# 250 blocks instead of 252 in a graph attention kernel: block bounds chosen from two candidates, expert groups of three first and two last, the fallback's branch behind the last addition

## The chip, the core and the metric

The kernel runs on one core of one Trainium2 chip. Times are device microseconds of one execution; lower is better. A core has TensorE (PE, matmuls, with weight loads of its own), VectorE (DVE), ScalarE (ACT), GpSimd (POOL) and SyncE (SP, which here issues nearly all plain transfers). Each engine works through its own instructions in order, and they meet at semaphores.

## The reference

One layer: graph attention with relation types over 30000 nodes of 256 features and 510000 edges (480000 random ones and a loop at each node), and after it a mixture of experts. The edges come sorted by destination.

```python
feat_all = einsum('ni,rhid->rnhd', layernorm(x), conv_weights)   # 8 relations, 4 heads of 64
el = sum(feat_all[type, src] * attn_l[type]);  er = sum(feat_all[type, dst] * attn_r[type])
e = leaky_relu(el + er, 0.2)
alpha = softmax of e over the edges of one destination
h[dst] = sum(alpha * feat_all[type, src]) + h_bias
x = x + h
y = layernorm(x)
out = x + shared_mlp(y) + sum of the 2 best of 4 experts, weighted by a softmax of their gates
```

## The kernel before, in words

There are two stages and a fallback.

Stage 1 goes over 235 tiles of 128 rows. Each is normalised, turned, and multiplied by the weights of all relations and heads (`group`, L304, six PSUM buffers); the rows go to `feat` in device memory, with the source half of the score as a 65th column of each head. Between these matmuls the program places side work, a step at a time: the generator `edge_records` (packs edges into records and finds the bounds of the blocks), then `places` (prepares each block's indices and flags, in batches of 12 blocks), then the loads of the experts' weights. `aside()` takes one step per row tile while `edge_records` runs and two afterwards. From row tile 178 on `first_rows` gathers one row per partition of each block ahead (L632) and stores these to `stage`, at a pace spread over the remaining tiles and never ahead of what `places` has made ready.

Stage 2 goes over `NBLK + 1` blocks. A block owns whole nodes: all edges of at most 128 nodes, and at most `CAP` = 2048 edges, 16 for each partition. Block t begins at the first node whose edges begin at or after `t * S`, found in a window of `WN` = 64 edges (L433 to L440: `miss` marks edges of the same node as the one before, a minimum finds the first other one). The last block, t = NBLK, is different: it takes the last 18 x 128 edges and the last 128 nodes. `bad` gathers the cases in which this doesn't hold (a block with too many edges or nodes, edges not sorted, and others).

The order of stage 2 is written by hand: t counts blocks, and each t has six slots, c = 0 to 5. In slot 0 of t come the loads of block t + 2 and the gathers of block t + 1: 15 indirect transfers (18 in the last block), issued by POOL at L962, into a ring `ft` of four blocks. Block t itself has its scores in slot 1 (L1066), the ends of its rows turned in slot 2 (L993), a scan across partitions (L1084), turned back (L1091), and softmax and exponentials in slot 5 (L1107). In the next t its rows are weighed (L1115) and summed by matmuls with one-hot matrices (`sums`, L1122), and `finish` divides by the denominator (`den`, L1144). In slot 0 of t + 2 `residual_sum` adds x (L1157) and takes the statistics of the second layernorm (L739).

The experts work on groups of `T` = 4 blocks. When a group's last block is added, its steps (`Experts.steps`) go to the end of the list `todo`, and each slot takes one of them, two from t = NBLK on. The steps are `spread` (L744), two `scale` (L749 to L754), two `turn` (L762), `shared1` and `gates`, four `experts1`, `shared2`, two `experts2`, two `weigh`, `turn_gates`, and one `last` for each block of the group (L871 to L877: matmuls into a PSUM tile with one buffer, the addition that ends the block, and its output transfer). What a step returns is called `late` and runs before the next step. With 253 blocks there are 62 groups of four, then one of three, then one of two.

After stage 2 comes the fallback, a slower method for inputs that don't fit: three loops (L1224, L1300, L1414) whose count is a multiple of `again`, read from `bad` at L1222. With `bad` = 0 they run zero times. `bad` is complete in stage 1, and each engine passes these loops at the place where the program puts them among its instructions.

Of the kernel before, what the change touches and what calls it, by code (L numbers as in the profile page):

```python
# [10 lines left out]
F32 = mybir.dt.float32  # L11
# [10 lines left out]
P = 128  # L22
# [11 lines left out]

U = 16
CAP = U * P
S = 2016
UL = 18  # L40
T = 4

# [14 lines left out]
def kernel(  # L57
# [48 lines left out]
    thr_d = dram.tile([NBLK, 2, P], F32, name="thr_d")  # L106
    exc_d = dram.tile([P], F32, name="exc_d")
    KT = -(-(NBLK + 1) // P)
    lo_d = dram.tile([KT, P], F32, name="lo_d")
    n_d = dram.tile([KT, P], F32, name="n_d")  # L110
    uns_d = dram.tile([EP], F32, name="uns_d")
    mnmx = dram.tile([2, NGRP], F32, name="mnmx")
    lohi_d = dram.tile([NT, 2], I32, name="lohi_d")

# [9 lines left out]
    nbc = const.tile([P, NBLK], F32, name="nbc")  # L124
    rowid = const.tile([P, NBLK + 1], F32, name="rowid")
    bad = const.tile([1, 1], I32, name="bad")
    lohi = const.tile([1, NT * 2], I32, name="lohi")
    hb = const.tile([P, D], F32, name="hb")

# [91 lines left out]
    with ExitStack() as cx:  # L221
# [123 lines left out]
        def edge_records(cl):  # L345
# [11 lines left out]
            for c in range(nch):  # L357
# [8 lines left out]
                else:  # L366
                    nc.vector.memset(d_sb[:, 0:1], -1)
                    nc.sync.dma_start(d_sb[:, 1:], dstv[:, :n])
                    with nc.allow_non_contiguous_dma(reason="one edge of each partition, once"):
# [32 lines left out]
                              zx.bitcast(BF16)[:, :R * 3 * H])  # L402
            yield


            WN = 64
            FAR = float(1 << 23)
            dw = gp.tile([P, KT, WN + 1], I32, name="dw")
            nc.gpsimd.memset(dw, -1)
            jj = gp.tile([P, WN], F32, name="jj")  # L410
            nc.gpsimd.iota(jj, pattern=[[1, WN]], base=0, channel_multiplier=0,
                           allow_small_or_imprecise_dtypes=True)
            first = gp.tile([P, KT], F32, name="first")
            irow = gp.tile([P, 1], F32, name="irow")
            nc.gpsimd.iota(irow, pattern=[[0, 1]], base=0, channel_multiplier=1,
                           allow_small_or_imprecise_dtypes=True)
            yield
            for k in range(KT):
                nc.vector.tensor_scalar(first[:, k:k + 1], irow, float(S), float(k * P * S), op0=ALU.mult,
                                        op1=ALU.add)  # L420
            nc.sync.dma_start(dw[0:1, 0, 1:], dst[0:WN].rearrange("(o c) -> o c", o=1))
            for k in range(KT):
                a = 1 if k == 0 else 0
                n = min(P, NBLK + 1 - k * P)
                nc.sync.dma_start(dw[a:n, k, :],
                                  bass.AP(tensor=dst.tensor, offset=dst.offset + (k * P + a) * S - 1,
                                          ap=[[S, n - a], [1, WN + 1]]))
            before_last = gp.tile([1, 1], I32, name="before_last")
            nc.sync.dma_start(before_last, dst[E - UL * P - 1:E - UL * P].rearrange("(o c) -> o c", o=1))
            yield  # L430
            lof = gp.tile([P, 2, KT], F32, name="lof")
            miss = gp.tile([P, KT, WN], F32, name="miss")
            nc.vector.tensor_tensor(miss, dw[:, :, 1:], dw[:, :, :WN], op=ALU.is_equal)  # L433
            yield
            for i, v in enumerate((jj[:, None, :].to_broadcast([P, KT, WN]), dw[:, :, 1:])):
                cand = gp.tile([P, KT, WN], F32, name="cand")
                nc.vector.scalar_tensor_tensor(cand, miss, FAR, v, op0=ALU.mult, op1=ALU.add)
                nc.vector.tensor_reduce(lof[:, i, :], cand, AX.X, ALU.min)
                yield
            nc.vector.tensor_add(lof[:, 0, :], lof[:, 0, :], first)  # L440
            nc.vector.tensor_scalar_min(lof[:, 0, :], lof[:, 0, :], float(E))
            nc.vector.tensor_scalar(lof[:, 1, :], lof[:, 1, :], 0.0, float(N), op0=ALU.max, op1=ALU.min)
            yield
            lor = gp.tile([1, KT * P], F32, name="lor")
            nr = gp.tile([1, KT * P], F32, name="nr")
            with nc.allow_non_contiguous_dma(reason="first edges and nodes of blocks, once"):
                for i, (t_d, row) in enumerate(((lo_d, lor), (n_d, nr))):
                    nc.sync.dma_start(t_d.rearrange("k p -> p k"), lof[:, i, :])
                    yield
                    if i:  # L450
                        nc.sync.dma_start(t_d[0:1, 0:1], zx[0:1, 0:1])
                        yield
                    nc.sync.dma_start(row, t_d.rearrange("(o k) p -> o (k p)", o=1))
                    yield
            nc.vector.tensor_copy(lo_sb, lor)
            nc.vector.tensor_copy(n_sb, nr)
            nc.vector.tensor_scalar_min(n0_sb, nr, float(N - P))
# [1 line left out]
            yield  # L459
            nc.vector.tensor_scalar(rowid[:, :NBLK], nbc, irow, None, op0=ALU.add)  # L460
            nc.vector.tensor_scalar_add(rowid[:, NBLK:], irow, float(N - P))
            unm = gp.tile([EP, 1], F32, name="unm")
            nc.vector.tensor_reduce(unm, uns, AX.X, ALU.max)
            yield
            with nc.allow_non_contiguous_dma(reason="one number of each partition, once"):
                nc.sync.dma_start(uns_d.rearrange("(p o) -> p o", o=1), unm)
            yield
            unr = gp.tile([1, EP], F32, name="unr")
            nc.sync.dma_start(unr, uns_d.rearrange("(o p) -> o p", o=1))


            two = gp.tile([1, 5], F32, name="two")
            gap = gp.tile([1, NBLK], F32, name="gap")
            for i, (row, most) in enumerate(((lor, CAP), (nr, P))):
                nc.vector.tensor_sub(gap, row[:, 1:NBLK + 1], row[:, :NBLK])
                nc.vector.tensor_reduce(two[:, i:i + 1], gap, AX.X, ALU.max)
# [4 lines left out]
            yield  # L481
            nc.vector.tensor_reduce(two[:, 4:5], unr, AX.X, ALU.max)
            nc.vector.tensor_reduce(bad, two, AX.X, ALU.max)

        BT = 3 * NT // 4
        count = {"ready": 0, "sent": 0}
# [395 lines left out]
    with ExitStack() as cx:  # L882
# [241 lines left out]

        groups = {}

        left, sizes = (NBLK + 1) % T, [T] * ((NBLK + 1) // T)
        sizes = sizes[:-1] + [T - 1, 2] if left == 1 else sizes + [left] if left else sizes[:-1] + [2, 2]
        member = [(sum(sizes[:q]), n) for q, n in enumerate(sizes) for _ in range(n)]
        todo = []  # L1130
        late = []
# [17 lines left out]
        def residual_sum(t):  # L1149
            s = blk.pop(t)  # L1150
            q, n = member[t]
            j = t - q
            if j == 0:
                x1 = x1p.tile([P, T, D], F32, name="x1")
                groups[q] = Experts(xc, ph_p, pc_p, x1, n, lambda i, r, q=q: put(q + i, r))
            x1 = groups[q].x1
            nc.vector.tensor_add(x1[:, j, :], s.ho.rearrange("p h d -> p (h d)"), s.xt)  # L1157
            groups[q].stats(j)
            if j == n - 1:
                todo.extend(groups.pop(q).steps())  # L1160

        with tc.manual_schedule():
            for t in range(-2, NBLK + 12):
                if t == 0:
                    for fb in fbs:
                        nc.vector.memset(fb, 0.0)

                def at(f, b, *a):  # L1170
                    if 0 <= b <= NBLK:
                        f(b, *a)
                for c in range(NCH):
                    while late:
                        late.pop()()
                    if c == 0:
                        at(load, t + 2)
                        at(gather, t + 1)
                        at(flags, t + 1)
                    if c == 1:  # L1180
                        at(flags_across, t + 1)
                    if c == 2:
                        at(turn_ends, t)
                    if c == 3:
                        at(across, t)
                    if c == 4:
                        at(turn_back, t)
                    if c == 5:
                        at(softmax, t)
                        at(exps, t)  # L1190
                        at(dest_pick, t + 2, 0)
                    if c == 4:
                        at(dest_select, t + 2)
                    if c < NCH - 1:
                        at(weigh, t - 1, c + 1)
                    if 0 < c < 4:
                        at(dest_pick, t + 1, c)
                    if c == 0:
                        at(residual_sum, t - 2)
                    if c == 1:  # L1200
                        at(scores, t)
                    for _ in range(2 if t >= NBLK else 1):
                        while late:
                            late.pop()()
                        if todo:
                            after = todo.pop(0)()
                            if after:
                                late.append(after)
                    if c == 5:
                        at(weigh, t, 0)  # L1210
                    if c == 4:
                        at(dest_expand, t + 2, 0)
                    if c < 3:
                        at(dest_expand, t + 1, c + 1)
                    at(onehot, t, c)
                    at(sums, t - 1, c)
                    if c == 5:
                        at(finish, t - 1)
            assert not todo and not groups and not late


    again = nc.values_load(bad[0:1, 0:1], min_val=0, max_val=1)  # L1222
    with tc.tile_pool(name="gr2", bufs=1) as gp, tc.tile_pool(name="ed2", bufs=2) as ep:
        with tc.For_i(0, again):  # L1224
            mn = gp.tile([EP, GPP], F32, name="mn")
# [228 lines left out]
```

## Time and profile before

| | us |
|---|---|
| median of three runs (lowest, highest) | 8487.05 (8483.83, 8509.22) |
| the profiled execution | 6603.28 |
| its span, first to last instruction | 6601.5 |
| PE busy in the span | 6047.9 (92%) |
| DVE busy | 5254.8 (80%) |
| POOL busy | 4082.8 (62%) |
| ACT busy | 3405.3 (52%) |
| mean granted clock of TensorE | 0.971 |

The runs are longer than the profiled execution by 1884 us. The profile describes the latter alone.

A row of a group gives line, engine, operation, tiles, and after the bar its busy time, the mean time of one in ns, and the idle time of the engine before it with what ended it. In a timeline the columns are start, duration, engine and line, and in brackets the idle time before and what ended it. `issue` is time in which the engine waited for nothing that the profile shows. A letter q behind an engine's name (POOLq) is its queue, where branches, semaphores and transfers are issued; these don't count as busy.

### The profile page before, as it was taken

How to read it: one execution, taken by the hardware profiler on the slowest of the kernel's cores; microseconds unless marked ns; L12 is line 12 of the kernel's file. 1: busy time of each engine (PE TensorE's matmuls, PEld its weight loads, DVE VectorE, ACT ScalarE, POOL GpSimd, SP SyncE). 2: the span in 40 equal slices, each digit the busy share in tenths (PEclk: the TensorE clock that was granted, in tenths of full speed). 3: DMA queues.
4: the chain of work that ended last, by engine and by line, in shares of the span. 5: the costliest groups of instructions: out<-in, count | busy, mean ns of one | idle time of the engine just before them, and what ended most of it. 6: DMA issues, size and time to landing. Idle time of an engine off the chain costs nothing. (4 is left out here: it accounts for less than half of the span.)

```text
span 6601.5 us, 97367 instructions
## 1 busy us (share of the span) xinstructions
PE 6047.9 (92%) x25770; PEld 3891.0 (59%) x25771; DVE 5254.8 (80%) x13699; ACT 3405.3 (52%) x8758; POOL 4082.8 (62%) x4424
## 2 busy tenths in 40 slices
PE   9999999999689989989899998899899999988998
PEld 5555555555356666666666666666666666666665
DVE  5555767644488888898888898898888888888895
ACT  2222222222256566666666665666656666566664
POOL 1111111266677777777777777777777777777773
PEclk9999999999899999999999999999999999999998
DMA  6666676799855555555555555555555555555552
GB/s 228 226 210 200 226 238 225 247 337 330 267 160 163 161 164 163 163 163 160 165 163 163 160 164 165 163 160 161 164 162 167 158 163 164 163 165 159 163 163 74
DMA packets 764586, 1214.72 MB, mean 184 GB/s; under 512 B 242498, under 2 KB 602917, under 8 KB 733813
## 3 DMA queue, kind: packets, MB, share of 16 engines
q1 hardware_dynamic: 568581, 668.72, 31.4%
q0 software_dynamic: 194400, 539.40, 29.3%
q8 instruction: 209, 3.42, 0.2%
q14 instruction: 356, 2.92, 0.1%
q10 hardware_dynamic: 1040, 0.26, 0.0%
HBM read 821.54 MB, written 386.43 MB: 183 GB/s over the span
## 5 line engine op out<-in xcount | busy, mean ns | idle before, releaser
L962 POOL DMA_INDIRECT ft<-feat,rk x3798 | 3606.7, 950 | 1169.0 <-issue 390.3
L1122 PE MATMUL po<-ft,oh 128*128 128x260 f32 x8100 | 2189.0, 407 | 137.1 <-DVE ho L1147 128.6
L1122 PEld LDWEIGHTS po<-ft,oh 128*128 128x128 f32 x8100 | 1520.4, 201 | 433.8 <-issue 196.5
L304 PE MATMUL ps<-w,xT 128*128 128x448 f32 (+1 forms) x4700 | 1708.4, 519 | 2.0 <-DMA w<-_L_gnn_conv_weights_dram 2.0
L1115 DVE TENSOR_TENSOR ft<-ft,p 128x768 f32<-128x768 f32 x1518 | 1292.2, 852 | 90.0 <-ACT ft L1108 86.1
L1049 ACT ACTIVATE oh<-icol,rk 128x128 f32<-128x128 f32 x4032 | 1327.7, 389 | 0.0
L304 PEld LDWEIGHTS ps<-w,xT 128*128 128x128 f32 x4700 | 875.6, 190 | 689.1 <-issue 603.3
L306 ACT COPY fo<-ps 128x448 f32<-128x448 f32 (+1 forms) x711 | 378.0, 533 | 1062.5 <-PE ps L304 972.5
L1050 ACT ACTIVATE oh<-oh 128x384 f32<-128x384 f32 x1518 | 741.1, 488 | 48.1
L1026 PEld LDWEIGHTS <-ohT 128*128 128x128 bf16 x4050 | 378.2, 158 | 408.9 <-issue 332.6
L1039 DVE TENSOR_REDUCE e<-ere 128x16 f32<-128x384 f32 (+1 forms) x1012 | 561.3, 555 | 34.6
L1037 DVE TENSOR_TENSOR ere<-pe,rk 128x384 f32<-128x384 f32 x1008 | 550.8, 546 | 1.3 <-PE pe L1026 1.3
L1107 ACT ACTIVATE p<-e 128x64 f32<-128x64 f32 (+1 forms) x253 | 70.2, 277 | 839.2 <-DVE e L1061 808.1
L1026 PE MATMUL pe<-erp,ohT 128*128 128x96 bf16 x4050 | 438.8, 233 | 60.5 <-DVE ohT L1009 37.5
L818 PE MATMUL ph<-xT,v 128*128 128x512 f32 (+2 forms) x1024 | 490.3, 602 | 0.4 <-ACT a L819 0.4
L306 DVE COPY fo<-ps 128x448 f32<-128x448 f32 (+1 forms) x464 | 242.3, 527 | 200.4 <-PE ps L304 194.1
L293 DVE COPY xT<-ptr 128x256 f32<-128x256 f32 x229 | 97.0, 424 | 368.6 <-PE ptr L291 367.0
L632 POOL DMA_INDIRECT fr<-feat,lowc x252 | 239.7, 951 | 193.7 <-DMA stage<-fr 90.2
L1009 DVE TENSOR_SCALAR ohT<-dr,rowid 128x2064 bf16<-128x2064 int16 (+1 forms) x253 | 323.6, 1279 | 19.8 <-DMA stage<-fr 19.7
L273 POOL TENSOR_TENSOR xb<-xg,hb 128x1024 f32<-128x1024 f32 (+1 forms) x59 | 140.7, 2385 | 272.1 <-DMA xg<-in_x_dram 161.9
L993 PE MATMUL t<-ident,fb 128*8 128x128 f32 x506 | 104.3, 290 | 214.9 <-DVE fb L1072 214.7
L819 ACT ACTIVATE a<-ph,c 128x512 f32<-128x512 f32 (+2 forms) x256 | 173.6, 678 | 195.7 <-PE ph L818 195.7
(219 smaller groups left out, 6810.9 us busy)
## 6 DMA issues: line engine op xcount, KB each, us to landing
feat<-fo SPq DMA_DIRECT2D x234, 1040.0 KB
dr<-dk_d SPq DMA_DIRECT2D x252, 516.0 KB
ft<-feat,rk POOLq DMA_INDIRECT x3798
stage<-fr SPq DMA_DIRECT2D x84, 390.0 KB
ft<-stage SPq DMA_DIRECT2D x252, 130.0 KB
xt<-xb_d SPq DMA_DIRECT2D x253, 128.0 KB
out_dram<-og SPq DMA_DIRECT2D x253, 128.0 KB
xb_d<-xb SPq DMA_DIRECT2D x58, 512.0 KB
```

Of the source, the lines that this page charges most:

```text
L304: nc.tensor.matmul(ps, t["xT"][:, k, :], w[:, k, c0:c1], start=k == 0, stop=k == 1)
L306: eng(t["fo"][:, h0:h1, :HD], ps[:, :n].rearrange("p (a d) -> p a d", d=HD))
L818: nc.tensor.matmul(ps[:, :self.w], lhs, rhs, start=i == 0, stop=i == len(pairs) - 1)
L962: nc.gpsimd.indirect_dma_start(out=s.ft[:, u].rearrange("p h d -> p (h d)"), out_offset=None, in_=feat[:, :], in_offset=bass.IndirectOffse ...
L1009: nc.vector.tensor_scalar(ohT[:, :3 * s.dw].rearrange("n (i e) -> n i e", i=3), s.dr[:, :, :s.dw], rowid[:, t:t + 1], None, op0=ALU.is_equal)
L1026: nc.tensor.matmul(pe[:, u - u0].rearrange("p f r -> p (f r)"), s.ov[:, u, :], s.erp.rearrange("n h k r -> n (h k r)"), start=True, stop=True)
L1037: nc.vector.tensor_mul(ere, s.pe[:, :u1 - u0], s.th[:, u0:u1, None, :].to_broadcast([P, u1 - u0, H * 3, R]))
L1039: nc.vector.tensor_reduce(s.e[:, :, u0:u1].rearrange("p h u -> p u h"), ere.rearrange("p u (h k) r -> p u h (k r)", h=H), AX.X, ALU.add)
L1049: nc.scalar.activation(s.oh[:, u, :], icol, AF.Abs, bias=s.nd[:, u:u + 1])
L1050: nc.scalar.activation(s.oh[:, u0:u1], s.oh[:, u0:u1], AF.Relu, bias=1.0, scale=-1.0)
L1115: nc.vector.tensor_mul(fc, fc, pc[:, :, None].to_broadcast([P, (u1 - u0) * H, HD]))
L1122: nc.tensor.matmul(s.po.rearrange("n h d -> n (h d)"), s.oh[:, u, :], s.ft[:, u].rearrange("p h d -> p (h d)"), start=u == 0, stop=u == s. ...
```

## The change

`S`, the distance of the blocks' nominal starts, goes from 2016 to 2032, so `NBLK` from 252 to 250.

The bounds are found in another way. The window now reaches 64 edges back too, and there are two candidates for each bound, the last start of a node before `t * S` and the first at or after it. A scan over the blocks (`late`) takes the later one where the block before it still fits, and the earlier one otherwise. The candidates go through device memory once, as four rows (`cand_d`), in place of two round trips for `lo_d` and `n_d`, and the choice is made on one partition. The tiles of this part are in a pool of their own that is closed at its end; the generator has more steps.

The groups of the experts are sized the other way round: what is left over comes first (a group of three with 251 blocks), then fours, then two groups of two. Two steps per slot are taken in t = NBLK - 2, NBLK - 1, NBLK and from NBLK + 2 on, and one in NBLK + 1. When the last block is added, the first three steps of its group (`spread` and both `scale`) go ahead of what is still in `todo`. From t = NBLK on, what a step returns is held until the next step is taken rather than run at the slot's start.

At the end of stage 2 VectorE copies `bad` to `redo`, behind its last addition, and `again` is read from `redo`.

```diff
-S = 2016
+S = 2032
@@ edge_records
-            dw = gp.tile([P, KT, WN + 1], I32, name="dw")
+            dw = bp.tile([P, KT, 2 * WN + 1], I32, name="dw")
...
-            nc.vector.tensor_tensor(miss, dw[:, :, 1:], dw[:, :, :WN], op=ALU.is_equal)
-            yield
-            for i, v in enumerate((jj[:, None, :].to_broadcast([P, KT, WN]), dw[:, :, 1:])):
-                cand = gp.tile([P, KT, WN], F32, name="cand")
-                nc.vector.scalar_tensor_tensor(cand, miss, FAR, v, op0=ALU.mult, op1=ALU.add)
-                nc.vector.tensor_reduce(lof[:, i, :], cand, AX.X, ALU.min)
-                yield
+            nc.vector.tensor_tensor(miss, dw[:, :, 1:], dw[:, :, :2 * WN], op=ALU.is_equal)
+            yield
+            for i, v in enumerate((jj[:, None, :].to_broadcast([P, KT, 2 * WN]), dw[:, :, 1:])):
+                for f, (far, op) in enumerate(((-FAR, ALU.max), (FAR, ALU.min))):
+                    w2 = slice(f * WN, (f + 1) * WN)
+                    cand = bp.tile([P, KT, WN], F32, name="cand")
+                    nc.vector.scalar_tensor_tensor(cand, miss[:, :, w2], far, v[:, :, w2], op0=ALU.mult, op1=ALU.add)
+                    nc.vector.tensor_reduce(lof[:, i, f, :], cand, AX.X, op)
+                    yield
...
+                for k in range(4):
+                    nc.sync.dma_start(cand_d[k].rearrange("k p -> p k"), lof[:, k // 2, k % 2, :])
+                    yield
+                yield
+                nc.sync.dma_start(cands.rearrange("o i k -> o (i k)"),
+                                  cand_d.rearrange("(o i) k p -> o (i k p)", o=1))
...
+            for f in range(2):
+                for i, most in enumerate((CAP, P)):
+                    gap = bp.tile([1, NBLK], F32, name="gap")
+                    nc.vector.tensor_sub(gap, cands[:, 2 * i + 1, 1:NBLK + 1], cands[:, 2 * i + f, :NBLK])
+                    if i == 0:
+                        nc.vector.tensor_scalar(may[:, f], gap, float(most), None, op0=ALU.is_le)
+                    else:
+                        nc.vector.scalar_tensor_tensor(may[:, f], gap, float(most), may[:, f], op0=ALU.is_le,
+                                                       op1=ALU.mult)
+                yield
+            nc.vector.tensor_scalar_add(may[:, 1], may[:, 1], -1.0)
...
+            nc.vector.tensor_tensor_scan(late[:, 1:NBLK + 1], may[:, 1], may[:, 0], 1.0, ALU.add, ALU.max)
...
+            for i, row in enumerate((lor, nr)):
+                nc.vector.tensor_sub(row, cands[:, 2 * i + 1], cands[:, 2 * i])
+                nc.vector.tensor_mul(row, row, late)
+                nc.vector.tensor_add(row, row, cands[:, 2 * i])
+                yield
+            nc.sync.dma_start(n_d.rearrange("(o k) p -> o (k p)", o=1), nr)
...
@@ groups
-        left, sizes = (NBLK + 1) % T, [T] * ((NBLK + 1) // T)
-        sizes = sizes[:-1] + [T - 1, 2] if left == 1 else sizes + [left] if left else sizes[:-1] + [2, 2]
+        left = (NBLK + 1) % T
+        sizes = [left] * (left > 0) + [T] * ((NBLK + 1) // T - 1) + [2, 2]
...
-                todo.extend(groups.pop(q).steps())
+                steps = groups.pop(q).steps()
+                if t == NBLK:
+                    todo[:0] = steps[:3]
+                    steps = steps[3:]
+                todo.extend(steps)
...
-            for t in range(-2, NBLK + 12):
+            for t in range(-2, NBLK + 6):
...
+                steps = 2 if NBLK - 2 <= t != NBLK + 1 else 1
                 for c in range(NCH):
-                    while late:
+                    while late and t < NBLK:
                         late.pop()()
...
-                    for _ in range(2 if t >= NBLK else 1):
+                    for _ in range(steps):
...
             assert not todo and not groups and not late
-    again = nc.values_load(bad[0:1, 0:1], min_val=0, max_val=1)
+            nc.vector.tensor_copy(redo, bad)
+    again = nc.values_load(redo[0:1, 0:1], min_val=0, max_val=1)
```

## The prediction, made before the changed kernel had run

> **What bounds the kernel now.** First I read the busy times of the engines stretch by stretch, because the page's shares average two stages with different limits. The columns are PE, weight loads, DVE, ACT, POOL (busy us, instructions in brackets), granted clock, DMA share, GB/s.
>
> ```profile
> 400.00:600.00 200.00, 200.00 (x604) 108.69 (x603) 106.49 (x317) 51.62 (x110) 17.04 (x24) 1.00 0.58 186
> 1400.00:1600.00 200.00, 200.00 (x603) 108.63 (x602) 95.72 (x282) 51.48 (x109) 125.69 (x124) 1.00 0.96 330
> 3000.00:4000.00 1000.00, 902.56 (x4325) 616.50 (x4325) 888.61 (x2291) 621.37 (x1639) 757.17 (x798) 0.97 0.57 162
> 4000.00:5000.00 1000.00, 904.74 (x4315) 617.22 (x4313) 887.83 (x2278) 621.08 (x1638) 757.13 (x798) 0.97 0.57 163
> ```
>
> Up to about 1730 us (projection to feat) PE has no gap. In the block stage PE and DVE stand at 90% and 89%, POOL at 76% only, and yet POOL is the bound. That shows in the groups by line and in POOL's timeline:
>
> ```profile
> L962 POOL DMA_INDIRECT ft<-feat,rk x3798 | 3606.7, 950 | 1169.0 <-issue 390.3
> ```
>
> ```profile
> 1750.34 0.94 POOL L962 DMA_INDIRECT ft<-feat,rk  x1 [12.04 <-DMA erp<-erp_d]
> 1751.59 0.95 POOL L962 DMA_INDIRECT ft<-feat,rk  x1 [0.30 <-issue]
> ...
> 6511.85 0.95 POOL L962 DMA_INDIRECT ft<-feat,rk  x1 [0.31 <-issue]
> 6513.10 0.95 POOL L962 DMA_INDIRECT ft<-feat,rk  x1 [0.30 <-issue]
> ```
>
> Each gather is 0.95 us and is followed by 0.30 us that no buffer causes: whichever engine is named as releaser, the gap is 0.30. From 1750.34 to 6514.05 us 3798 gathers run without a hole, (6514.05 - 1750.34) / 3798 = 1.254 us each. A block of 15 gathers is 18.8 us. So blocks, not matmuls, set this stage, and 87.5 us (6601.5 - 6514.05) come after the last gather.
>
> Third, the timeline of that tail:
>
> ```profile
> 6558.65 0.16 DVE L1144 TENSOR_SCALAR den<-po 128x4 f32<-128x4 f32 x1 [3.79 <-PE po L1122]
> ...
> 6562.39 0.43 DVE L739 BATCH_NORM_STATS2 c_st<-x 128x6 f32<-128x256 f32 x1 [2.25 <-SPq L1224]
> ...
> 6565.24 0.15 DVE L749 RECIPROCAL c_rs<-c_rs 128x2 f32<-128x2 f32 x1
> ...
> 6591.66 2.07 PE L873 MATMUL pf<-v,a 128*128 128x256 f32 x4 [5.75 <-issue]
> ...
> 6594.92 0.42 DVE L877 TENSOR_TENSOR og<-pf,x 128x256 f32<-128x256 f32 x1 [9.77 <-PE pf L874]
> 6595.38 0.36 SPq L1139 DMA_DIRECT2D out_dram<-og  x1
> ```
>
> The loops of the fallback (L1224, L1300, L1414, run zero times) stand inside the last block's chain: DVE waits 2.25 us at the first, PE 5.75 us at the second. In the records of lines, PE's own branch of L1300 lasts 3748 ns.
>
> **What the Trainium skill says.** "Runtime: NRT & Kernel Launch", section Instruction fetch mechanics: fetching is sequential, and a taken branch to a far target waits for a fetch. The 3748 ns agrees. "TensorE: Matmul & The Clock Gate", Part 1: after an idle window of about 3.4 us TensorE falls to half clock until it has been busy as long. The trace agrees: granted clock is 1.00 until 6560, 0.50 from 6565 to 6575, 0.79 and 1.00 after it, and 0.50 again from 6590, each time behind a branch.
>
> **The change part by part**, against the profiled execution (span 6601.5 us, 6603.28 with what lies around it).
>
> *Two blocks fewer.* S from 2016 to 2032 makes ceil((510000 - 2048) / S) 250 instead of 252. That is 30 gathers x 1.254 = -37.6 us on the bounding queue. Work of other engines goes too and was covered. The gathers behind `stage` are two fewer, beside PE's full stage 1; their pace is spread over the same row tiles, so their end stays: 0 (+-2).
>
> *Bounds.* A block may hold 2048 edges. I worked the rules out on the reference's seeded `dst`. The old rule at S = 2032 would overfill 5 blocks, up to 2052 edges; the new one moves 7 boundaries back and its largest block has exactly 2048 edges and 126 nodes, so the fallback isn't taken. The cost is on DVE in stage 1: two more pairs on 128x128 elements (about 0.28 per operation, L433), and on one partition eight operations for `may`, one addition, six for `lor` and `nr`, 0.40 each (L475, L476), and a scan of some 0.7 (L572 takes 0.57 for 204 elements): 1.1 + 6.0 + 0.7 = about 8 us. DVE is half idle there and PE full with six PSUM buffers in flight: cost 0, and 8 us if that cover failed. SP issues four writes, a read and a write in place of five DMAs; feat stores queue behind them with seven `fo` buffers. About 11 more side steps, one per row tile of 1729 / 235 = 7.4 us, push `places` 80 us later, from an end near 1288 to near 1370 us. The first L632 gathers (1308.8 us) then run beside its last batches; they follow what is ready and have until 1738 us to catch up: 0, at worst +3.
>
> *Steps moved, up to the last block's sums.* Group sizes go from 62 fours, three, two to three, 61 fours, two, two. PE time of a group of four, from 2000 to 6000 us over 53 groups: (409.5 + 199.2 + 99.6 for L818, 219.7 + 148.5 + 144.0 for `last`, 114.4, 98.0, 97.7, 66.6) / 53 = 30.1 us, of it 9.7 in four `last`. From the last block's scores to its `den` 41.5 us pass now (6517.20 to 6558.65), filled on PE with two `last` of a four (4.8), the three's other steps (0.75 x 30.1 - 2.4 = 20.2), 31 sums (8.2) and turns (1.5): 34.7. Afterwards a two without its `last` (10.2), sums and turns: 19.9, so 14.8 less. But the last four's 22 steps now run doubled in two earlier slots: 30.1 us of PE instead of some 21.5, 8.6 more, where PE has about 4 us of slack in two blocks. The scores come late by that; gathers don't, as a ring slot is free some 17 us before its gather. Net -6; ends 0 (the last scores as late as the PE sum says, the chain bound by ACT and DVE) and -12.
>
> *The last group's chain*, `den` to the last addition: 6558.65 to 6595.34 = 36.7 us. `spread` and `scale` (ACT: table load 1.28, Sqrt 0.29, two scalings 1.09; DVE: 0.31) go ahead of two `last` (PE 2.4 each; DVE 0.42; an output DMA on SP, 0.36, hidden as 20 us follow). The 2.25 us at the branch and 1.6 us in which L749 stood behind an og addition go; late next is `turn`, behind the second `last` on PE, which waits for DVE through the one pc buffer: 1.8 back. Net -2. The 5.75 us stall and the half clock behind it (2.07 against 1.03, 1.22 against 0.69) go: -7.3. `last` also keeps PE at work ahead of `turn`, so some of the half-clock stretch goes: -2; 0 to -5, as an idle window may still fall there. Sum -11; ends -8 and -15.
>
> *Branch behind the last addition.* Every engine's register load now waits for the copy to `redo`. Behind it stand POOL's iotas (0.56) and the constants, nothing of the output. After the addition, one after another: copy and its signal 0.2, load 0.54, L1224 2.8 (6560.3 to 6563.1), constants 0.6, L1300 5.7 (SP there 6585.7, PE away 6591.4), L1414 2.8 (6595.9 to 6598.7), close 2.8: 15.4, less some overlap 15.0. Now 6.2. Cost +8.8; ends +5 (fetches overlap when all engines arrive together) and +14 (each engine pays its own). No row shows the three in series.
>
> Sum: -37.6 - 6 - 11 + 8.8 = -45.8, a span of 6555.7 us.
>
> **To the runs.** Their median is 8487.05, 1884 us above the profiled execution, and no view shows where this lies. If it is fixed, the gain stays 46 (8441). If all scales by 8487.05 / 6603.28 = 1.285, it is 59 (8428). If it is all per block, 1884 / 253 = 7.4 each, it is 46 + 15 = 61 (8426). I take 54: 8433.
>
> **Rivals.**
> - *The tail gives nothing.* Group chain and sums stay as long and the branches cost 8.8: -37.6 + 8.8 = -29, 8450 to 8458. For: PE sums move forward, they don't vanish, and the branches in series are unmeasured. Against: the 5.75 us stall is there to be removed.
> - *More than the profile shows.* The runs' blocks are 26 us each (18.8 + 7.4), and the tail at its good ends (-12, -15, +5) is scaled too: -53 - 28 = -81, 8406. For: the unexplained 28%. Against: nothing says that it is per block.
> - *Slower: the fallback runs.* Place: `bad` at L1222. It decides from one block above 2048 edges or 128 nodes. Price: all 510000 edges gathered again, 3984 x 1.254 = 5.0 ms at least, so over 13400. For: the largest block has no edge to spare. Against: my count, on whole numbers that float32 holds.
>
> **How the numbers follow.** Forecast 0.62, tail gives nothing 0.18, more 0.12, fallback 0.05, something unseen of either sign 0.03. The forecast's own range, from its ends and both scalings, is 8410 to 8462; with the two neighbours and the runs' own scatter (8483.83 to 8509.22) 8396 to 8470, which leaves out the fallback and the far ends. A difference under 0.3% (25 us) can't be told from none. The tail rival straddles that line. Faster: 0.60 + 0.10 + 0.12 = 0.82; same 0.11; slower 0.07.
>
> **What would show it.** 3768 gathers at L962, still 0.30 apart, the last ending near 6476 us: right on the main step. `den` of the last block some 38 us later, no wait at a loop's line before the last addition, some 15 us after it. Wrong: gathers that start later than 1755 us, gaps above 0.30 in the last four blocks (the ring ran full), over 40 us from last gather to `den`, or work at L1300's loop body.

## The result, and the profile after

The changed kernel takes 8461.31 us (median of 14 runs, 8425.74 to 8483.99) where the kernel before takes 8503.72 (14 runs, 8483.83 to 8527.46) beside it: a ratio of 0.9953, 95% interval 0.994 to 0.9967. That is 40 us less (0.0047 x 8503.72) where 54 were forecast.

One thing must be known to read the numbers: each set of runs was wholly at one of two levels, near 6600 us or near 8500 us, the kernel before included (its profiled execution of 6603 us was of the lower level, its runs of the upper one), so ratios are taken inside a set, and lines of two traces are compared at the same level or in stage 1 and the tail, which both levels share.

The stretches of the changed kernel's profiled execution (upper level; the columns are as before):

```profile
400.00:600.00 200.00, 200.00 (x603) 108.59 (x602) 108.84 (x320) 51.51 (x110) 17.98 (x16) 1.00 0.62 193
1400.00:1600.00 200.00, 200.00 (x602) 108.42 (x601) 88.76 (x279) 50.08 (x108) 126.03 (x122) 1.00 0.97 334
3000.00:4000.00 1000.00, 737.40 (x3150) 492.06 (x3149) 655.29 (x1662) 453.37 (x1193) 542.35 (x573) 0.85 0.41 118
4000.00:5000.00 1000.00, 718.77 (x3058) 476.68 (x3057) 635.11 (x1622) 440.93 (x1160) 545.40 (x575) 0.84 0.40 117
```

The two stretches of stage 1 look as before. In the block stage no engine is near full: this is the upper level, not the change (the kernel before, traced at that level, has PE busy 721.96 us of the first thousand). The groups by line name the gathers and, new, a wait in the matmuls of stage 1:

```profile
L998 POOL DMA_INDIRECT ft<-feat,rk x3768 | 3576.6, 949 | 2989.4 <-PE po L1158 1486.9
...
L306 PE MATMUL ps<-w,xT 128*128 128x448 f32 (+1 forms) x4700 | 1709.6, 519 | 14.9 <-ACT thr L637 13.5
```

The same kernel ran again in a set at the lower level (`all_again` below). POOL's timeline there answers to that of before:

```profile
1773.41 0.94 POOL L998 DMA_INDIRECT ft<-feat,rk  x1 [9.00 <-DMA stage<-fr]
1774.66 0.94 POOL L998 DMA_INDIRECT ft<-feat,rk  x1 [0.30 <-issue]
```

```profile
6494.24 0.95 POOL L998 DMA_INDIRECT ft<-feat,rk  x1 [0.30 <-PE ph L891]
6495.49 0.95 POOL L998 DMA_INDIRECT ft<-feat,rk  x1 [0.30 <-issue]
```

3768 gathers, (6496.44 - 1773.41) / 3768 = 1.253 us each: the bound and its price held, 30 gathers fewer. But the first starts at 1773.4 instead of 1750.3, and from the end of the last one to the `den` of the last block, at 6543.9, it is 47.5 us, where before has 44.6 (6558.65 - 6514.05).

The tail of the changed kernel's profiled execution:

```profile
8404.56 0.16 DVE L1181 TENSOR_SCALAR den<-po 128x4 f32<-128x4 f32 x1 [2.25 <-PE po L1158]
...
8405.89 0.43 DVE L775 BATCH_NORM_STATS2 c_st<-x 128x6 f32<-128x256 f32 x1
...
8406.89 0.17 DVE L785 RECIPROCAL c_rs<-c_rs 128x2 f32<-128x2 f32 x1 [0.36 <-ACT c_rs L780]
...
8427.62 1.03 PE L909 MATMUL pf<-v,a 128*128 128x256 f32 x4
...
8429.30 0.42 DVE L913 TENSOR_TENSOR og<-pf,x 128x256 f32<-128x256 f32 x1 [2.28 <-PE pf L910]
8429.64 0.13 DVE L1263 COPY redo<-bad 1x1 int32<-1x1 int32 x1
8429.76 0.34 SPq L1176 DMA_DIRECT2D out_dram<-og  x1
```

`den` to the end of the last addition is 8429.72 - 8404.56 = 25.2 us instead of 36.7. The wait at the branch and the half clock of L909 are gone (1.03 us in place of 2.07). From there to the end of the span, 8450.3, it is 20.6 us instead of 6.2.

### The profile page after: what moved, and what is told of

It is laid out like the page before. It is cut to its first block, busy times and chain, and to the rows that moved or that the text cites. A ratio compares the mean times of both kernels' runs of the same rounds, so it can differ in the third digit from the quotient of the medians.

```text
span 8450.3 us, 96821 instructions
## 1 busy us (share of the span) xinstructions
PE 6512.4 (77%) x25626; PEld 4133.3 (49%) x25627; DVE 5270.1 (62%) x13647; ACT 3391.0 (40%) x8706; POOL 4054.1 (48%) x4392
## 5 line engine op out<-in xcount | busy, mean ns | idle before, releaser
L1158 PE MATMUL po<-ft,oh 128*128 128x260 f32 x8036 | 2404.5, 440 | 349.2 <-DVE ho L1184 114.6
L1158 PEld LDWEIGHTS po<-ft,oh 128*128 128x128 f32 x8036 | 1647.2, 219 | 720.2 <-issue 428.1
L1075 DVE TENSOR_REDUCE e<-ere 128x16 f32<-128x384 f32 x1004 | 557.0, 555 | 34.5
L1143 ACT ACTIVATE p<-e 128x64 f32<-128x64 f32 x251 | 69.6, 277 | 1265.3 <-DVE e L1097 1146.8
L854 PE MATMUL ph<-xT,v 128*128 128x512 f32 (+2 forms) x1024 | 508.8, 622 | 0.0
L800 ACT COPY xT<-ph 128x512 f32<-128x512 f32 (+2 forms) x128 | 73.1, 571 | 1077.0 <-remote 719.2
L854 PE MATMUL ph<-xT,w 128*128 128x512 f32 (+2 forms) x512 | 348.4, 808 | 201.8 <-issue 140.5
L907 PE MATMUL pf<-w,h 128*128 128x256 f32 x502 | 203.4, 494 | 299.5 <-ACT wT L900 147.8
L1045 DVE TENSOR_SCALAR ohT<-dr,rowid 128x2064 bf16<-128x2064 int16 x251 | 321.2, 1280 | 18.2 <-DMA feat<-fo 16.6
```

The costliest lines, as they stand in the source:

```text
L854: nc.tensor.matmul(ps[:, :self.w], lhs, rhs, start=i == 0, stop=i == len(pairs) - 1)
L1045: nc.vector.tensor_scalar(ohT[:, :3 * s.dw].rearrange("n (i e) -> n i e", i=3), s.dr[:, :, :s.dw], rowid[:, t:t + 1], None, op0=ALU.is_equal)
L1075: nc.vector.tensor_reduce(s.e[:, :, u0:u1].rearrange("p h u -> p u h"), ere.rearrange("p u (h k) r -> p u h (k r)", h=H), AX.X, ALU.add)
L1158: nc.tensor.matmul(s.po.rearrange("n h d -> n (h d)"), s.oh[:, u, :], s.ft[:, u].rearrange("p h d -> p (h d)"), start=u == 0, stop=u == s. ...
```

## The experiments

Two things stood against the prediction from the first trace on: stage 1 is some 20 us longer, and the close is longer than the branch was to cost. Every kernel below ran beside the kernel before.

### The parts of the change, at the lower level

Here the kernel before takes 6600.8 us. Three kernels undo parts of the change; the fourth is the change itself.

```diff
blocks_only: old groups and order, old place of the branch
-            nc.vector.tensor_copy(redo, bad)
...
-    again = nc.values_load(redo[0:1, 0:1], min_val=0, max_val=1)
+    again = nc.values_load(bad[0:1, 0:1], min_val=0, max_val=1)
blocks_branch: old groups and order, new place of the branch
blocks_groups: new groups and order, old place of the branch
all_again: the kernel after, unchanged
```

> The change with the old grouping and the old place of the branch: two blocks fewer and the new bounds alone. Theory A (a block costs what it costs in the trace of the changed kernel, 26.2 us from one den to the next): 2 x 26.2 = 52 less than the kernel before, ratio 0.9938. Theory B (a block costs its 15 gathers, 18.8 us, and nothing else of the 26.2 goes with it): 38 less, ratio 0.9956. In its trace PE stalls behind the loop at the second loop's line again, some 6 us, and about 6 us pass from the last addition to the end.

> Blocks and the branch behind the last addition, old grouping (its last group has three blocks). My sum: the stalls in the last chain go (2.25 and 5.75 us, and the half clock behind them), the three loops in series come behind the last addition: 15 us there by my prediction, 20.6 as the changed kernel's trace has it. Net against blocks alone 0 by the first figure, +6 by the second. Rival (the branch costs nothing, engines that arrive together overlap): 8 us less than blocks alone.

> Blocks, the new grouping and order, the branch in its old place. My sum: 6 us less up to the last block's den and some 4 in the chain behind it, so about 10 less than blocks alone, with PE's stall at the second loop's line still there and about 6 us from the last addition to the end. Rival (doubled steps in two earlier slots only move PE's work): no gain up to den, 0 to 4 less in all.

> The changed kernel itself, beside its parts on the same chip: 0.9953 of the kernel before as measured, some 40 us less. If the parts add up, it is blocks alone plus the branch's difference plus the grouping's. Theory A with these small parts gives 45 to 60 less; theory B 35 to 45 less.

| kernel | median us | ratio (95%) | first gather | first gather to last `den` | last `den` to last addition | last addition to end |
|---|---|---|---|---|---|---|
| before | 6600.8 | | 1750.3 | 4808.3 | 36.7 | 6.2 |
| blocks_only | 6591.53 | 0.9984 (0.9978 to 0.9991) | 1776.2 | 4768.4 | 38.7 | 13.6 |
| blocks_branch | 6590.1 | 0.9981 (0.9972 to 0.999) | 1774.8 | 4766.8 | 32.1 | 20.6 |
| blocks_groups | 6591.74 | 0.9987 (0.998 to 0.9994) | 1770.9 | 4768.0 | 36.8 | 12.0 |
| all_again | 6591.1 | 0.9982 (0.9976 to 0.9989) | 1773.4 | 4770.5 | 26.5 | 20.4 |

(The last four columns are from the timeline of one profiled execution each; the first gather and `den` are taken at their starts.) None gains what was expected over before: each gains about 10 us, and neither the branch nor the groups make a difference beyond the intervals (for the branch that is the first figure of its text, for the groups the rival). The columns say why. The two blocks pay in full (4808.3 - 4768.4 = 39.9). But all four start their gathers 21 to 26 us late, and even with the old branch the close is 6 to 7 us longer.

### Why stage 1 is longer

The waits of PE from 1300 to 1740 us, in the changed kernel (us, times, longest):

```profile
PE ps L306 <- ACT thr L637: 13.5, 1, 13.5
PE ptr L293 <- DVE a_xn L148: 5.6, 4, 1.8
```

At the end of `places`, ACT copies `thr` twice into a tile with one buffer, and the second copy waits until the store of the first has landed. The copies and the store between them in a second trace of the kernel before, `before_again`, and in the changed kernel:

```profile
1280.59 0.38 ACT L601 COPY thr<-ps 128x256 f32<-128x256 f32 x1
1280.99 3.53 SPq L603 DMA_DIRECT2D thr_d<-thr  x1
1287.62 0.37 ACT L601 COPY thr<-ps 124x256 f32<-124x256 f32 x1 [6.66 <-DMA thr_d<-thr]
```

```profile
1359.86 0.38 ACT L637 COPY thr<-ps 128x256 f32<-128x256 f32 x1
1377.46 1.32 SPq L639 DMA_DIRECT2D thr_d<-thr  x1
1383.05 0.37 ACT L637 COPY thr<-ps 122x256 f32<-122x256 f32 x1 [22.81 <-DMA thr_d<-thr]
```

The same wait is three times as long when it falls at 1360 us instead of 1281. The store itself is no slower, it has landed 6.6 us and 5.6 us after its start; but in the changed kernel SP starts it 17.6 us after the copy, behind other transfers in its order. Behind ACT stand the copies that free PE's PSUM buffers. Three kernels ask what the cause is. `thr2` takes the wait away by a second buffer, `merged` does the same work in eleven steps fewer, `late_before` adds eleven empty steps to the kernel before.

```diff
thr2
-                thr = gp.tile([P, 2 * P], F32, name="thr")[:n]
+                thr = gp.tile([P, 2 * P], F32, name="thr", bufs=2)[:n]
merged: 11 fewer (2 in the candidates, 4 in the writes, 1 after the read, 2 in may, 2 in lor and nr), such as
                     nc.sync.dma_start(cand_d[k].rearrange("k p -> p k"), lof[:, k // 2, k % 2, :])
-                    yield
late_before
             nc.vector.tensor_reduce(bad, two, AX.X, ALU.max)
+            for _ in range(11):
+                yield
```

> The kernel after, with two buffers for the tile thr in place of one. Seen before: in all_again the copy into thr at L637 waits 23.8 us for the store of the first copy to land, PE stands 14.5 us behind it, and stage 1 ends 25 us later than before. Theory A (the one buffer is what the delay costs): that wait goes, PE's stall of 14.5 us and most of the 7.1 us at L293 after it go with it, stage 1 ends at 1733 to 1740 us instead of 1755, the span is 6569 to 6577, 15 to 22 us under all_again's 6590.8. Theory B (transfers pushed into the stretch where the DMA engines are already full are the cost, the buffer only shows it): PE loses the same time a little later, waiting for row tiles of x; stage 1 still ends at 1750 or later and the span is 6586 to 6592.

> The kernel after, with the same work of the bounds in 11 side steps fewer (eleven yields taken out), so that places starts and ends as early as before; thr keeps one buffer. Theory A and theory B (the delay of places is the cost, by the buffer or by the transfers): thr is copied near 1281 us, stage 1 ends at 1729 to 1734 us, the span is 6564 to 6572, some 22 us under all_again, and the ratio to before is about 0.995. Theory C (the bounds' own work on DVE and SP is the cost): stage 1 still ends near 1750 us, the span is 6586 to 6592.

> The kernel before with eleven empty side steps at the end of edge_records, nothing else: 252 blocks, old bounds. Theory A or B (the delay alone costs it): thr is copied near 1361 us, stage 1 ends at 1748 to 1756 us, the span is 6618 to 6628, 0.3 to 0.4% over before. Theory C (the bounds' work): no change, 6601. A second question: POOL's last drain took 1.88 us in before and 7.92 us in every kernel with 250 blocks. If the count of gathers sets it, it is 1.88 us here too; if it varies from one execution to the next, it may be anything.

This set came out at the upper level (before 8503.03 us), so the spans expected don't apply; the ends of stage 1 and the ratios do. `before_again` and `after` are of other sets at that level.

| kernel | ratio (95%) | second `thr` copy, us | stage 1 ends, us | first gather, us |
|---|---|---|---|---|
| before_again | 0.9998 (0.9987 to 1.0009) | 1287.6 | 1730.3 | 1748.9 |
| after | 0.9953 (0.994 to 0.9967) | 1383.0 | 1750.4 | 1768.3 |
| thr2 | 0.9947 (0.9933 to 0.9962) | 1363.5 | 1749.6 | 1768.3 |
| merged | 0.9928 (0.9912 to 0.9944) | 1285.7 | 1729.0 | 1740.6 |
| late_before | 1.0035 (1.0024 to 1.0047) | 1387.2 | 1753.6 | 1775.0 |

`late_before` has none of the new bounds and loses as much: 0.0035 x 8503 = 30 us (20 to 40 by the interval). `merged` has all of them, and stage 1 ends as early as in `before_again`. So the delay is the cost and not the bounds' own work; theory C falls. Between A and B `thr2` decides against A. Its stall at `thr` is gone, and stage 1 still ends at 1749.6. PE loses the time piece by piece:

```profile
PE ptr L293 <- DVE a_xn L148: 14.4, 7, 4.1
```

and that goes back to row tiles of x that come late, as DVE's waits of `thr2` from 1300 to 1760 us show (5.5 us in `before_again`):

```profile
DVE a_st L141 <- DMA xg<-in_x_dram: 54.6, 9, 8.3
```

So the buffer was only one place where the lag showed. How the lag reaches x is seen in one round of four row tiles, first in `merged`, then in `thr2`. In the program POOL's addition of the bias (`xb`) follows the statistics of the second tile; SP stores `xb` and only then loads the next four tiles of x:

```profile
1440.38 0.42 DVE L141 BATCH_NORM_STATS2 a_st<-xg 128x6 f32<-128x256 f32 x1
1441.18 2.35 POOL L275 TENSOR_TENSOR xb<-xg,hb 128x1024 f32<-128x1024 f32 x1
1444.58 0.73 SPq L252 DMA_DIRECT2D xg<-in_x_dram  x1
```

```profile
1449.92 0.42 DVE L141 BATCH_NORM_STATS2 a_st<-xg 128x6 f32<-128x256 f32 x1
1468.07 2.36 POOL L275 TENSOR_TENSOR xb<-xg,hb 128x1024 f32<-128x1024 f32 x1
1470.89 0.69 SPq L252 DMA_DIRECT2D xg<-in_x_dram  x1
1478.05 0.43 DVE L141 BATCH_NORM_STATS2 a_st<-xg 128x6 f32<-128x256 f32 x1 [5.23 <-DMA xg<-in_x_dram]
```

The load takes 7.2 us to land in `thr2`, but it starts 20.6 us after those statistics, in `merged` 3.8. Most of that is POOL's addition, which stands in POOL's order behind gathers of `first_rows`, and these wait for a buffer whose store to `stage` hasn't landed (79.5 us in `thr2` from 1380 to 1750 us, 58.5 in `merged` from 1380 to 1730). What the transfers have to pass through is seen in two stretches of `merged` and then of `thr2`, with the DMA share and GB/s in the last columns:

```profile
1200.00:1300.00 100.00, 100.00 (x306) 54.52 (x305) 64.06 (x172) 25.76 (x56) 13.48 (x27) 1.00 0.74 239
1300.00:1400.00 100.00, 100.00 (x303) 54.44 (x302) 44.02 (x144) 26.09 (x55) 55.87 (x54) 1.00 0.96 332
```

```profile
1200.00:1300.00 100.00, 100.00 (x303) 54.38 (x302) 71.23 (x182) 25.15 (x53) 17.91 (x39) 1.00 0.68 222
1300.00:1400.00 100.00, 100.00 (x307) 54.69 (x306) 60.16 (x166) 26.52 (x57) 50.29 (x67) 1.00 1.01 292
1400.00:1700.00 300.00, 285.35 (x840) 152.96 (x840) 130.45 (x396) 68.49 (x152) 187.75 (x183) 0.98 0.98 336
```

Before 1300 us a quarter of the DMA engines' time is free; after it next to none is, because the gathers and stores of `first_rows` run until the end of the stage. The last batches of `places` moved across that line. Over the first 1400 us `merged` moves 232 GB/s and `thr2` 226, so `thr2` is 6 x 1400 = 8.4 MB behind, 5.7 of them since 1200 us (1.7 and 4.0 from the lines above). At 336 GB/s, which both move from there to 1700 us, that is an estimated 25 us; stage 1 ends 20.6 us later than in `merged`. PE shows the same: it idles 14.65 of the next 300 us, and its granted clock of 0.98 there costs it an estimated 6 us more. The Trainium skill, "DMA: Bandwidth & Descriptors", section "Issuing engines are not separate DMA queues", says that transfers started by ScalarE, SyncE or GpSimd run on the same 16 DMA engines and interleave. The trace agrees: from 1300 to 1760 us of `thr2` the queue of the plain transfers takes 75.3% of the 16 engines' time and that of the gathers 22.7%.

So the delay as the cost is shown by `late_before` and `merged`. That full DMA engines are what makes it cost is argued from these rates. A rival stays open: that the orders of POOL and SP, in which x stands behind gathers and stores, would hold it up with free DMA engines too. No run gave `xb` or the loads of x an engine of their own.

### Why the close is longer

POOL's last instruction of any length is a DRAIN. Its durations (ns, shortest, median, longest) in before, in `blocks_only` and in the changed kernel:

```profile
L1450 POOLq DRAIN  x3: 40/103/1877, 6598.8 to 6601.2; - x3
```

```profile
L1487 POOLq DRAIN  x3: 40/103/7920, 6588.1 to 6596.6; - x3
```

```profile
L1494 POOLq DRAIN  x3: 40/103/7920, 8441.5 to 8450.0; - x3
```

It is 6.04 us longer in the last two, though `blocks_only` has the old branch. What the two share is two blocks fewer: 3768 + 250 = 4018 gathers where before has 3798 + 252 = 4050. `gathers32` adds 32 gathers that nothing reads, one per row tile in stage 1.

```diff
...
+                    if g == 3 and 10 <= m < 42:
+                        nc.gpsimd.indirect_dma_start(
+                            out=gp.tile([P, D], F32, name="idle_rows"), out_offset=None, in_=x[0:N, :],
+                            in_offset=bass.IndirectOffsetOnAxis(ap=spare[:, 0:1], axis=0))
```

> The kernel after with 32 more indirect gathers (128 rows of x each, read by nothing) on POOL, one per row tile from tile 10 to 41, so that POOL issues as many in the whole as the kernel before (4018 / 2 + 32 = 2041 against 4050 / 2 = 2025, counted as the trace lists each twice; the total isn't equal, so only a dependence on the total can be seen, not its exact rule). Theory D (the place in POOL's descriptor ring sets its last drain): the drain is no longer 7.92 us and INC_SWDGE_SEM no longer 2.10; the time from the last addition to the end changes with it, from 20.4 us. Theory E (something else of the 250-block kernels sets it): 7.92 and 2.10 again, 20.4 us again, span as all_again.

The halving in that text is wrong: the trace lists each gather once, and with 32 more the total is 4050, as before. Measured: ratio 0.9948 (0.9932 to 0.9964), and

```profile
L1500 POOLq DRAIN  x3: 40/103/1877, 8446.4 to 8448.8; - x3
```

with INC_SWDGE_SEM, POOL's instruction in the second skipped loop, at 0.62 us again (2.10 in the changed kernel) and 12.4 us from the last addition to the end, instead of 20.6. `late_before`, with 252 blocks, has 1877 ns too. So this drain depends on how many gathers POOL has issued in the whole, as theory D has it. The rule behind it isn't known: two totals were tried, and no run shows a ring of descriptors at work.

### The parts again, with the delay gone

The last set was at the upper level again (before 8529.63 us).

```diff
before_again: the kernel before, unchanged
blocks_merged: blocks_only with the yields of merged taken out
groups_merged: blocks_groups with the yields of merged taken out
best2: merged, the 32 gathers of gathers32, and one loop for the fallback
...
+    with tc.For_i(0, again):
...
-        with tc.For_i(0, again * NT) as t:
+            with tc.For_i(0, NT) as t:
...
-        with tc.For_i(0, again * NQ) as q:
+            with tc.For_i(0, NQ) as q:
```

> The kernel before once more, for a second trace of it, on the chip of the next three runs. Both theories: ratio 1.000. If this chip is at the 8500 us level, its trace is the first of the kernel before there: a block takes some 26.2 us instead of 18.8, stage 1 ends near 1730 us, the time from the last addition to the end is 6.1 us with a last POOL drain of 1.88.

> The two blocks alone (old groups, old place of the branch) with the eleven side steps merged. Theory (two blocks at full price, stage 1 as long as before, the last drain 6 us longer): span under before by two block periods less 6 us, so -32 us at the 6600 level (ratio 0.995) or -46 at the 8500 level (0.9946). Rival (a part of the loss lies elsewhere in the new bounds): no better than blocks_only, -5 to -10 us, ratio 0.9985.

> As blocks_merged, with the new group sizes and the order of steps, and the branch in its old place. The prediction's step (-6 up to the last den, and of the -11 behind it the -2 that need no branch): 8 us under blocks_merged. Rival (the four steps doubled in two earlier slots give back what is moved): equal to blocks_merged within 3 us, as blocks_groups was to blocks_only.

> The kernel after with the eleven side steps merged, 32 spare gathers on POOL in stage 1 as in gathers32, and the fallback in one loop (three skipped loops become one). Theory (stage 1's delay, the drain and the loops passed in series are three separate losses that add up): stage 1 ends at 1729 us, the last drain is 1.88, the last addition to the end 20.4 - 7.4 - 6 = 7 us, so 20 to 28 + 13 us under after: some 8415 at the 8500 level (ratio 0.990) or 6553 at the 6600 level (0.993). Rival (one loop is passed as slowly as three, since each engine fetches at the far end anyway): 12.4 us after the last addition.

| kernel | median us | ratio (95%) | stage 1 ends | last `den` to last addition | last addition to end |
|---|---|---|---|---|---|
| before_again | 8526.05 | 0.9998 (0.9987 to 1.0009) | 1730.3 | 36.6 | 6.1 |
| blocks_merged | 8484.54 | 0.9944 (0.9928 to 0.996) | 1729.2 | 38.7 | 13.1 |
| groups_merged | 8463.65 | 0.993 (0.9914 to 0.9946) | 1729.2 | 37.2 | 11.5 |
| best2 | 8470.88 | 0.9924 (0.9907 to 0.9942) | 1729.6 | 26.5 | 9.5 |

`blocks_merged` came out as expected: 48 us (0.0056 x 8530) for two blocks less the longer drain. `groups_merged` is 12 us under it, but their intervals overlap, and at the lower level the same pair without the merging differed by 0.2 us; the groups' share stays unclear. `best2` closes in 9.5 us, between the 7 and the 12.4 expected: one loop saves 2.9 us on `gathers32`, not 6. Its ratio is the lowest measured, but its interval overlaps that of `merged`, so the shorter close isn't shown in the run's time. Both lie under the changed kernel's 0.9953, with intervals that overlap its own at the edge.

## Why the prediction was right, and where it was wrong

The direction and the main term held; the total gain was smaller than forecast, 40 us for 54. At the lower level, whose profile the prediction was made against, the sum was to be -45.8 us and one profiled execution of the changed kernel shows -10.7 (6601.5 to 6590.8):

| term | predicted | measured |
|---|---|---|
| two blocks and steps moved (first gather to last `den`) | -37.6 - 6 | -37.8 |
| delay of `places` (first gather) | 0, at worst +3 | +23.1 |
| last group's chain | -11 | -10.2 |
| close | +8.8 | +14.2 |

*Two blocks: right.* 39.9 us in `blocks_only` for 37.6.

*Bounds' own work, 0: right.* `merged` does it all, and stage 1 ends at 1729.0 us.

*"About 11 more side steps ... push places 80 us later ... 0, at worst +3": wrong, and the step that failed.* The delay itself was predicted well (`thr` at 1281 moved to 1360). But I asked only whether the gathers of `first_rows` could follow, not what the moved steps carry. They carry megabytes into a stretch where, in a line that I had shown myself, the DMA share stood at 0.96. `late_before` against before gives the delay's price alone, 30 us. `merged` ends stage 1 21 us before `after`; in the time of the runs the two differ by as much, (0.9953 - 0.9928) x 8503 = 21 us, but across two sets and with intervals that overlap a little, and against `thr2` of its own set by 16 us, which isn't clear of noise. The sign named for it, gathers that start later than 1755 us, is what the trace showed.

*Steps moved, -6: not seen.* First gather to last `den` is 4768.4 without the new order and 4768.0 with it: the end named 0. The sign of being wrong that was named here came too, over 40 us from the last gather to `den`: 47.5 where 38 were forecast.

*Last group's chain, -11: right.* -10.2. From `blocks_only`, where it is 38.7, the order alone takes 1.9 (predicted 2), the branch alone 6.6 and both together 12.2. The prediction also found that the trace of before agrees with a half clock that lasts until PE has been busy for some 3.4 us. For its end that isn't so: PE works from 6566.3 us on with hardly a gap, and the granted clock of 0.79 from 6575 to 6580 puts the end of the half clock at 6577, some 11 us later.

*Branch, +8.8: right by itself, the close wrong.* With the branch alone moved the close grows by 20.6 - 13.6 = 7.0, with the new groups by 20.4 - 12.0 = 8.4; with the old drain, in `gathers32`, it is 12.4, 6.2 more than before. The rest is the drain of 7.92 us in place of 1.88 and INC_SWDGE_SEM of 2.10 in place of 0.62, 7.5 us together, which come with two blocks fewer and which no line of before let me expect. With it the close grew by 14.2 us, just past the end of +14 that I had put to the branch.

*To the runs: right in size, for a reason left open.* Of the three ways that I gave for the 1884 us, "all per block" is the one. `before_again` is the first trace of the kernel before at the upper level:

```profile
L962 POOL DMA_INDIRECT ft<-feat,rk x3798 | 3608.1, 950 | 3054.1 <-PE po L1122 1364.3
```

A gather is 950 ns as ever, but POOL stands 3054.1 us instead of 1169.0 before them. 8524.7 - 6601.5 = 1923 us over 253 blocks is 7.6 each, and a block takes 26.4 us. So two blocks were worth about 53 there, which made up for part of the 21 to 30 us lost in stage 1. That the forecast came near is partly luck: at the lower level the same kernel gains 10 us. And the pieces don't quite add up: 53 for the blocks and some 11 for the chain, less 20 for stage 1 and 14 for the close, is an estimated 30 us where 40 were measured.

What sets the level isn't known. `before_again` has waits that the trace of before doesn't have at all, ended by a signal that the trace ties to no instruction (`remote`). The two largest from 2000 to 6000 us (us, times, longest):

```profile
ACT xT L764 <- remote: 601.9, 37, 19.7
DVE car L1084 <- remote: 342.1, 31, 13.7
```

Both instructions read a tile that PE writes, so PE's results seem to come late at the upper level. The granted clock is 0.87 against 0.97, which may be a consequence of PE's idle time as well as a cause, and none of the runs was made to tell the two apart. The three sets of experiments also ran on three different chips, the one at the lower level on a chip of its own, so the level may belong to the chip.

## What to carry to other kernels

Before pushing a stream of side work later, ask what the stretch it is pushed into has left, for each resource that the work uses, its transfers too: here DVE and ACT had room for it and the DMA engines next to none, and half of the forecast gain (23 of 46 us at the lower level) was lost in it. A stall at a single buffer can be the place where a lag shows, not its cause; take the buffer away and see whether the end moves. Where side steps come at a fixed beat, each new one delays all that follow, so small ones are better merged: that alone ended stage 1 21 us earlier here, with no instruction removed.

## What the hardware showed that was not expected

- POOL's last DRAIN lasts 7.92 us in every traced kernel with 4018 gathers and 1.88 us in every one with 4050, whatever else they do.
- A DMA share of 1.01 carried 292 GB/s and one of 0.96 carried 332 GB/s in the same stretch of the two kernels above: the share alone doesn't tell how much is moved.
- PE's longest branch at the skipped loops lasted 3.3 to 4.0 us in every kernel (4044 ns in the changed one), and 3.8 us when three loops were made one.
- Two levels of time for one kernel, 6.6 and 8.5 ms, with the same duration of a gather on POOL (0.95 us) and the same stage 1 (it ends at 1729.6 and 1730.3 us in the kernel before).
